# A graph convolution and a mixture of experts on one core: column means taken out of the first weights, keys and constants moved forward, degree roots written as rows, router rows on VectorE, low parts on GpSimd

## The chip, the core and the metric

The kernel runs as one program on one core of a Trainium2 chip. Its time is device microseconds of one execution on that core. TensorE multiplies matrices, VectorE, ScalarE and GpSimd compute element by element, each with a queue of its own that it works off in order; SyncE issues most DMA transfers, GpSimd the indirect ones.

## The reference, cut to what matters

```python
x: [1250, 512]          # nodes x features, float32
src, dst: [41250]       # edges, both directions and one loop of each node, sorted by dst

def gcn_conv(x, W, b, src, dst, n):        # adds another loop of each node to s and d
    h = x @ W.T
    deg = zeros(n).at[d].add(1.0)
    dinv = where(deg > 0, deg ** -0.5, 0)
    msg = h[s] * (dinv[s] * dinv[d])[:, None]
    return segment_sum(msg, d, n) + b

h = layernorm(x)                           # no weights
h = relu(gcn_conv(h, W1, b1))              # 512 -> 128
z = gcn_conv(h, W2, b2)                    # 128 -> 64
y = relu(z @ Wd1.T + bd1)                  # 64 -> 128
y = relu(y @ Wd2.T + bd2)                  # 128 -> 256
x = x + y @ Wd3.T + bd3                    # 256 -> 512

g = layernorm(x)                           # of the first 512 rows
# 512 tokens, 2 of 8 experts each (with weights), hidden 256, exact gelu:
for e in range(8):  y[rows of e] = gelu(g[rows of e] @ w1[e]) @ w2[e]
x[:512] += sum over a token's two experts of weight * y
return x
```

## The kernel before

The 1250 nodes are ten tiles of 128 rows (the last has 98). Because `dst` is sorted, the edges into six neighbouring nodes stand together: a *group* is six nodes, there are 209 groups, and the core gathers for each a window of 256 edges (`sg`, `dg`, indirect DMAs on GpSimd). The graph is turned into a dense count matrix `T` (source by target). For a group, VectorE compares edge keys with a row of numbers and so writes one-hot rows: `om` says of each edge which of 128 rows its source is (`source_rows`, L493), `on0` and `on1` say the tile of the source and the target (`target_rows`, L493 too). TensorE multiplies them (`count`, L521 and L524), ScalarE copies the counts out of PSUM (L532).

This runs in 14 steps, called *supers*, of sixteen groups, k = 0 to 13. Each has two halves, and the order of the other work around the counts is written by hand: `plan[(k, 0)]` and `plan[(k, 1)]` are the steps issued behind the first and the second half's counts, `plan[(k, 2)]` and `plan[(k, 3)]` those behind the pieces of the layers that follow. The source rows of super k + 1 are issued ahead of the counts of the first half of super k, its target rows ahead of those of the second half. So everything that a plan gives to VectorE stands in its queue between one-hot rows, and TensorE counts no faster than these come. In the plan are:

- the layer norm and the first product, tile by tile: `statistics` (VectorE, L287 and the line behind it: mean and variance into `mv`), `center` (ScalarE, L297: `xc` is the mean less x), `turned` (TensorE transposes `xc`, L308, ScalarE copies it out, L310), `product` (four matmuls with `W1s`, L317; a PSUM bank holds `PER` = 4 tiles);
- the degrees: `degree_rows` and `degree_sums`, `degree_row` (six row products on TensorE and three Sqrt on ScalarE for `rrow`, the roots as one row), `degree_inverse` (VectorE, and two DMAs on SyncE, which write 1/root to DRAM as `line` and read it back as rows into `drow`);
- `deviations` (ScalarE: `sd`), `scales` (VectorE) and `scaled_parts` (ScalarE multiplies the products by their scale), for each bank;
- the router of the experts: `router_pairs`, `router_ranks`, `router_places` (GpSimd, many small instructions), `router_lists` and `router_tokens`.

The products of `T` are made in bf16 with an operand cut into three parts that add up to float32 precision. `cut` makes them: ScalarE copies the high part, VectorE subtracts it (`low`, L446), ScalarE copies the middle part (L447), VectorE subtracts again (L448). `cut_on`, called in each half, issues the cuts that are due, two at most. `first_layer` puts its pieces into a list from which `fill` issues some behind each half, from super 4 on (`LAYER` = 4, 6, 8, 10, 12 are the supers behind which another chunk of 384 or fewer columns is ready): a matmul with the bias row `b1r` and `rrow`, ten parts of three or four matmuls (L560), a Relu, then the second product and the cut of `h2` in three parts (`h2hm` holds high and middle, `h2lo` the low part). The second layer multiplies the parts of `h2` with `T` (`thick` and `thin` pieces); then come the decoders `decode1` to `decode3`.

Behind the one-hot rows, in front of the second layer, GpSimd adds the last bias to all ten tiles of `xs` (`add_last_bias`, L1026). `decode3` adds its product to `xs`: for tiles 0 to 3 ahead of the experts, for tiles 4 to 9 at the end.

The experts' stage: the normalised rows of the 512 tokens go to DRAM (`x2d`), GpSimd fetches each expert's rows by indirect DMA into a ring of five buffers (`fetch`, L1148). Expert 0 comes by a product instead (`first_rows`). Each expert has up to 128 tokens in a tile of its own, and what it has above that in a tile shared by four (tiles 8 and 9). The order of the fetches is 8, 1, 2, 3, 4, 9, 5, 6, 7: five at once, each of the others behind the turn of an earlier one (`second_turn`, L1161, TensorE), since it needs its buffer. `results` multiplies by the second weights, and GpSimd scatters the scaled rows into `results_d` (a memset, L1219, and the indirect DMA, L1220); at the end they are read back and added.

```python
    gathers = [fetch(fetched.pop(0)) for _ in range(XG)]
    for i, e in enumerate(range(WAHEAD, WAHEAD + MORE)):
        for n, f in ((1, load_first), (2, load_second)):
            behind(f(e), gathers[2 * i + n], "behind rows that are wanted sooner")
    decode2(*c1)
    fill(len(pieces) // 2)
    first_rows()
```

(This is the place in the kernel, behind `decode3` of tiles 0 to 3, where the first five fetches are issued.)

Of the kernel before, what the change touches and what calls it, by code (L numbers as in the profile page):

```python
# [15 lines left out]
P = 128  # L16
# [32 lines left out]
def sorted_path(  # L49
# [110 lines left out]
    W1s = const.tile([P, KD, HID], F32)  # L160
# [53 lines left out]
    mv = const.tile([P, NT, 2], F32)  # L214
    deg = const.tile([P, NT], F32)
    root = const.tile([P, NT], F32)
    dcol = const.tile([P, NT], F32)
    hs = graph.tile([P, NT, HID], F32)
    h2 = graph.tile([P, NT, LAT], F32)
    if NF < NT:  # L220
        edge = rows(NF) // 32 * 32
        nc.vector.memset(mv[edge:, NF, :], 1.0)
        nc.vector.memset(dcol[edge:, NF:], 1.0)
        nc.vector.memset(root[edge:, NF:], 1.0)
        nc.vector.memset(deg[edge:, NF:], 0.0)
        nc.vector.memset(hs[edge:, NF, :], 0.0)
        nc.vector.memset(h2[edge:, NF, :], 0.0)
    lates = [graph.tile([P, SG, NK], F16, name=f"on1_{i}") for i in range(3)]
    for late in lates:
        nc.gpsimd.memset(late, 0.0)  # L230

# [9 lines left out]
    for c in range(2):  # L241
# [18 lines left out]
        for a, to in ((dst, dg), (src, sg)):  # L260
# [7 lines left out]
            )  # L268

# [11 lines left out]
    PER = 512 // HID  # L281
    products = [held_bank(f"ph{j}") for j in range((NT + PER - 1) // PER)]

# [5 lines left out]

    xTs = {}  # L290

    centered = {}

    def center(t):
        r = rows(t)
        centered[t] = work.tile([P, D], F32, tag="xc", name=f"xc{t}")
        nc.scalar.activation(  # L297
            centered[t][:r], xs[:r, t, :], AF.Identity, bias=mv[:r, t, 0:1], scale=-1.0
        )

    def turned(t):
        r = rows(t)
        if t not in centered:
            center(t)
        xc = centered.pop(t)
        pt = bank(f"pt{t}").rearrange("p (k r) -> p k r", k=KD)
        for k in range(KD):
            nc.tensor.transpose(pt[:, k, :r], xc[:r, k * P : (k + 1) * P], ident[:r, :r])  # L308
# [3 lines left out]
    def product(t):  # L312
        r = rows(t)
        xT = xTs.pop(t)
        to = products[t // PER][:r, (t % PER) * HID : (t % PER + 1) * HID]
        for k in range(KD):
            nc.tensor.matmul(to, xT[:, k, :r], W1s[:, k, :], start=(k == 0), stop=(k == KD - 1))  # L317
# [64 lines left out]
    line = dram.tile([NT * P], F32, name="line")  # L382
# [34 lines left out]
    def degree_row():  # L417
        for c, w in chunks:
            pr = bank(f"pr{c}")
            for h in range(HT):  # L420
                nc.tensor.matmul(
                    pr[0:1, :w], ones16, nodes[:, h, c : c + w], start=(h == 0), stop=(h == HT - 1)
                )
            nc.scalar.activation(rrow[:, c : c + w], pr[0:1, :w], AF.Sqrt, bias=ones[0:1])

    def degree_inverse():
        nc.vector.reciprocal(dcol, root)
        nc.vector.tensor_mul(dcol2, dcol, dcol)
        nc.sync.dma_start(out=line.rearrange("(t p) -> p t", p=P), in_=dcol)
        nc.sync.dma_start(  # L430
            out=drow, in_=bass.AP(tensor=line.tensor, offset=line.offset, ap=[[0, P], [1, N]])
# [33 lines left out]
    def deviations(a, b):  # L465
        nc.scalar.activation(sd[:, a:b], mv[:, a:b, 1], AF.Sqrt, bias=eps)

    def scales(a, b):
        nc.vector.reciprocal(scale[:, a:b], sd[:, a:b])
        nc.vector.scalar_tensor_tensor(  # L470
            scale[:, a:b], scale[:, a:b], -1.0, dcol[:, a:b], op0=OP.mult, op1=OP.mult
        )

    def scaled_parts(j):
        ts = range(j * PER, min(NT, (j + 1) * PER))
        for t in ts:
# [3 lines left out]
                products[j][:r, (t - ts[0]) * HID : (t - ts[0] + 1) * HID],  # L480
# [3 lines left out]
        cut(hs[:, s, :], [q[:, s, :] for q in hp], f"h{j}", j < 2)  # L484
# [82 lines left out]

    def first_layer(c, w):
# [3 lines left out]
        def part(t):  # L572
            if t == 0:
                box["ps"] = bank(f"l1_{c}")
                nc.tensor.matmul(
                    box["ps"][:, :w], b1r, rrow[:, c : c + w], start=True, stop=False
                )
            spread(box["ps"], c, w, t, [(q, HID) for q in hp], False, t == NT - 1)
# [4 lines left out]
        def second():  # L583
# [13 lines left out]
            cut(h2[:, s, :], [h2hm[:, s, :LAT], h2hm[:, s, LAT:], h2lo[:, s, :]], f"g{c}")  # L597
# [45 lines left out]
    def late_constants():  # L643
        for c in range(2):
            nc.vector.tensor_copy(
                iota_d[:, c], iota_m[:, :GN].unsqueeze(1).broadcast_to([P, HT * CG, GN])
            )
        nc.vector.memset(iota_d[:, 0, CG:, :LATE], -1.0)
        nc.vector.memset(iota_d[:, 1, CG:LASTG, :LATE], -1.0)

    statistics(0)
    center(0)
    statistics(1)
    center(1)
    first_keys = keys(0)
    turned(0)
    turned(1)
    statistics(2)
    late_constants()
    first_keys = more_keys(0, *first_keys)  # L660
    turn_keys(0, *first_keys)
    late_keys = keys(1)
    center(2)
    product(0)
    product(1)
    made = {0: (source_rows(*supers[0]),)}
    statistics(3)
    turned(2)
    made[0] = (*made[0], *target_rows(*supers[0]))
    center(3)  # L670
    product(2)
    turned(3)
    late_keys = more_keys(1, *late_keys)
    statistics(4)
# [179 lines left out]

    def router_places():
# [46 lines left out]
        pool.tensor_add(chunks_of[:, :, 1], chunks_of[:, :, 1], none[:, :TT])  # L902
        in_chunk = const.tile([P, BL, ST], BF16, name="in_chunk")
        for b in range(BL):
            pool.tensor_scalar(
                at_row[:, b, :], iota_m, at[:, b : b + 1], None, op0=OP.is_equal
            )
            pool.tensor_scalar(
                in_chunk[:, b, :], iota_m[:, :ST], chunk[:, b : b + 1], None, op0=OP.is_equal
            )  # L910
        pool.tensor_tensor(
# [36 lines left out]
    zero = graph.tile([P, D], F32)  # L948

# [7 lines left out]
    def both(f, *ts):  # L957
# [3 lines left out]
    groups = [(a, min(NT, a + PER)) for a in range(0, NT, PER)]  # L961
    plan = {
        (0, 0): both(product, 3) + [lambda: turn_keys(1, *late_keys)] + both(center, 4),
# [785 lines left out]
```

## Time and profile before

| | |
|---|---|
| median of 9 runs | 173.95 us (171.91 to 175.53) |
| the profiled execution: its own time | 173.5 us |
| its span in the profile | 171.7 us |
| mean granted clock of TensorE | 0.972 |
| TensorE busy with matmuls | 139.9 us (81%), 1236 instructions |
| TensorE loading weights (beside them) | 99.5 us (58%) |
| VectorE busy | 98.7 us (58%) |
| ScalarE busy | 69.2 us (40%) |
| GpSimd busy | 104.1 us (61%) |

The span is the time between the first and the last recorded instruction; the execution's own time has 1.8 us around it. A share of busy time is a mean over stages with different limits: VectorE is busy without a pause in the first 73 us and little behind them, TensorE the other way round. In a view, "L493" is the line of the code, and an arrow as in `on<-iota_n,keys_n` leads from what is read to what is written. Rows of the timeline give the start and the duration of one instruction in us, in square brackets how long its engine had been idle before it and what ended that. In the windows, each engine has its busy time with the number of instructions in it, then come the granted clock (1.00 is full speed), the DMA engines' share and GB/s.

### The profile page before, as it was taken

What the parts mean: (1) busy time and instruction counts of PE and PEld (TensorE: products, weight loads), DVE (VectorE), ACT (ScalarE), POOL (GpSimd) and SP (SyncE); (2) the same over time, 40 slices, a digit from 0 to 9 for tenths busy, and PEclk for the clock granted to TensorE, in tenths of its full rate; (3) what the DMA queues carried; (4) which work ended last, traced back from release to release, by engine and by line L of the source; (5) the groups of instructions that cost most, each with busy time, mean ns of one, the idle gap of its engine ahead of it and who ended that gap; (6) DMA issues with size and microseconds to landing.
All of it is one profiled execution on the core that took longest, in us unless ns stands there. A gap on an engine that the chain in (4) does not pass through costs nothing.

```text
span 171.7 us, 3271 instructions
## 1 busy us (share of the span) xinstructions
PE 139.9 (81%) x1236; PEld 99.5 (58%) x1236; DVE 98.7 (58%) x180; ACT 69.2 (40%) x154; POOL 104.1 (61%) x168
## 2 busy tenths in 40 slices
PE   0059838869988898899999999989799999999800
PEld 0048828867566797786434459769465993445200
DVE  5799999991999999914465780240113010314930
ACT  3078594889834545533213265412311312121000
POOL 8589989994999999999998001757206101540000
PEclk9999996999999999999999999999999999999975
DMA  5978420102543456341000033479997920349990
GB/s 166 329 173 284 135 93 0 1 6 84 191 122 122 126 142 229 150 155 65 4 0 0 0 122 122 133 233 295 376 374 245 323 108 0 124 183 316 391 363 34
DMA packets 18366, 27.13 MB, mean 158 GB/s; under 512 B 4312, under 2 KB 9177, under 8 KB 18344
## 3 DMA queue, kind: packets, MB, share of 16 engines
q1 hardware_dynamic: 16596, 21.38, 37.8%
q0 software_dynamic: 1712, 5.41, 9.2%
q8 instruction: 11, 0.18, 0.5%
q14 instruction: 11, 0.09, 0.2%
q10 hardware_dynamic: 36, 0.06, 0.2%
HBM read 18.52 MB, written 8.33 MB: 156 GB/s over the span
## 4 chain that ended last, share of the span: by engine, by line
DVE 29%; PE 28%; issue 16%; DMA 9%; ACT 7%; POOL 5%; ACTq 1%; DVEq 0%; POOLq 0%; SPq 0%
DVE om L493 12%; PE l L560 7%; DVE on L493 5%; PE pd L1097 4%; POOL results_d L1220 4%; DMA xg<-x2d,tokens 3%; PE pf L1178 3%; PE eh L1195 3%; DMA win<-in_dst_dram 3%; DVE xs L1329 2%; DMA x<-results_d 2%; PE pt L308 2%; PE pd L1088 2%; DVE st L287 2%; ACT xc L297 2%
## 5 line engine op out<-in xcount | busy, mean ns | idle before, releaser
L493 DVE TENSOR_TENSOR om<-iota_m,keys_m 128x4096 f16<-128x4096 f16 (+1 forms) x14 | 29.9, 2138 | 0.0
L1220 POOL DMA_INDIRECT results_d<-y,targets x10 | 9.8, 978 | 24.5 <-ACT y L1216 15.8
L560 PE MATMUL l<-T,hp 128*128 128x192 bf16 (+5 forms) x180 | 20.3, 253 | 0.4 <-DVE hp L448 0.4
L308 PE MATMUL pt<-ident,xc 128*128 128x128 f32 (+1 forms) x40 | 7.5, 325 | 15.1 <-ACT xc L297 15.1
L532 ACT CAST T<-acc 128x480 bf16<-128x480 f32 (+1 forms) x27 | 14.7, 546 | 11.4 <-PE acc L524 10.4
L1211 PE MATMUL ey<-w,hT 128*128 128x512 f32 (+1 forms) x64 | 18.9, 598 | 0.0
L1195 PE MATMUL eh<-xgT,w 128*128 128x160 f32 x128 | 18.6, 300 | 0.0
L1097 PE MATMUL pd<-Wd3s,y 128*128 128x512 f32 (+1 forms) x40 | 18.0, 592 | 0.0
L1148 POOL DMA_INDIRECT xg<-x2d,tokens x9 | 8.7, 967 | 15.1 <-PE pf L1178 12.6
L1195 PEld LDWEIGHTS eh<-xgT,w 128*128 128x128 f32 x128 | 17.6, 190 | 0.2 <-issue 0.2
L560 PEld LDWEIGHTS <-hp 128*128 128x128 bf16 (+1 forms) x216 | 14.9, 97 | 3.6 <-issue 1.4
L521 PE MATMUL acc<-on,om 128*128 128x60 f16 x209 | 15.4, 190 | 0.1
L524 PE MATMUL acc<-on,om 128*128 128x60 f16 x209 | 15.1, 190 | 0.4 <-DVE on L493 0.4
L1218 DVE TENSOR_SCALAR y<-ey,wslot 128x512 f32<-128x512 f32 x5 | 3.8, 751 | 20.2 <-PE ey L1211 20.2
L308 PEld LDWEIGHTS pt<-ident,xc 128*128 128x128 f32 (+1 forms) x40 | 5.2, 164 | 16.0 <-issue 9.6
L521 PEld LDWEIGHTS <-om 128*128 128x128 f16 x209 | 13.7, 98 | 1.2 <-issue 0.8
L493 DVE TENSOR_TENSOR on<-iota_n,keys_n 128x960 f16<-128x960 f16 (+2 forms) x28 | 14.1, 542 | 0.0
L317 PE MATMUL ph<-W1s,xT 128*128 128x128 f32 (+1 forms) x80 | 12.7, 314 | 1.0 <-ACT xT L310 1.0
L524 PEld LDWEIGHTS <-om 128*128 128x128 f16 x209 | 12.7, 97 | 0.3 <-issue 0.2
L1026 POOL TENSOR_TENSOR xs<-xs,bd3s 128x512 f32<-128x512 f32 (+1 forms) x10 | 12.4, 1274 | 0.0
L317 PEld LDWEIGHTS ph<-W1s,xT 128*128 128x128 f32 (+1 forms) x80 | 11.6, 223 | 1.4 <-ACT xT L310 1.4
L1097 PEld LDWEIGHTS pd<-Wd3s,y 128*128 128x128 f32 (+1 forms) x40 | 7.5, 188 | 8.2 <-issue 7.7
(217 smaller groups left out, 275.0 us busy)
## 6 DMA issues: line engine op xcount, KB each, us to landing
w<-in_L_ffn_w_dram SPq DMA_DIRECT2D x16, 512.0 KB, 6.7
xs<-in_x_dram SPq DMA_DIRECT2D x9, 256.0 KB, 4.7
out_dram<-xs SPq DMA_DIRECT2D x9, 256.0 KB, 4.6
results_d<-zero SPq DMA_DIRECT2D x4, 512.0 KB, 2.7
x2d<-x SPq DMA_DIRECT2D x4, 256.0 KB, 2.0
x<-results_d SPq DMA_DIRECT2D x2, 512.0 KB, 4.0
got<-results_d SPq DMA_DIRECT2D x2, 512.0 KB, 5.4
win<-in_dst_dram SPq DMA_DIRECT2D x2, 336.0 KB, 3.7
```

Of the source, the lines that this page charges most:

```text
L308: nc.tensor.transpose(pt[:, k, :r], xc[:r, k * P : (k + 1) * P], ident[:r, :r])
L317: nc.tensor.matmul(to, xT[:, k, :r], W1s[:, k, :], start=(k == 0), stop=(k == KD - 1))
L493: nc.vector.tensor_tensor(to.rearrange("p j (a f) -> p j a f", f=4), iota.rearrange("p (a f) -> p a f", f=4).unsqueeze(1).broadcast_to([P, ...
L521: nc.tensor.matmul(acc[:, n0 : n0 + NK], om[:, (at + g) * HT, :], on0[:, at + g, :], start=True, stop=False)
L524: nc.tensor.matmul(acc[:, n0 : n0 + NK], om[:, (at + g) * HT + 1, :], on1[:, at + g, :], start=False, stop=True,)
L532: nc.scalar.copy(T[:, :, g0 * GN : (g0 + ng) * GN], acc[:, : ng * NK].rearrange("p (d t) -> p t d", t=NT),).ins
L560: nc.tensor.matmul(ps[row0 : row0 + m, a:b], s[:r, t, :m], moving, start=start and i == 0, stop=stop and i == len(order) - 1,)
L1026: pool.tensor_add(xs[:r, t, :], xs[:r, t, :], bd3s[:r])
L1097: nc.tensor.matmul(p3[:r], y2[c][:, k, t * P - c : t * P - c + r], Wd3s[:, k, :], start=(k == 0), stop=(k == K2 - 1),)
L1195: nc.tensor.matmul(ph[:, f, :], first_w[e][:, k, f * P : (f + 1) * P], xgT[:, k, e, :], start=(k == 0), stop=(k == KD - 1),)
L1211: nc.tensor.matmul(to, hT[e][:, f, a:b], second_w[e][:, f, :], start=(f == 0), stop=(f == KF - 1))
L1220: ins = pool.indirect_dma_start(out=results_d[:, :], out_offset=bass.IndirectOffsetOnAxis(ap=targets[:, j : j + 1], axis=0), in_=y, in_off ...
```

## The change

- The mean leaves the rows by way of the weights. `center_weights` multiplies `W1s` with a matrix of 1/512 (`portion`), which gives each column's mean in every row, and subtracts it: `W1c`. A 129th column of 1/512 makes the product give the row's mean besides. `center` is gone, `turned` transposes x itself, three tiles (`PER`) share a bank, and the tenth has a place of its own.
- `statistics` stays for tiles 0 to 2. For tiles 3 to 9 ScalarE copies the negative mean out of the product (`mean`) and takes the sum of squares of x less the mean (`square`, with `accum_out`).
- The four instructions for `iota_d` move ahead of the first keys, which stand right behind two turned tiles now.
- The scales come in two groups, tiles 0 to 5 at (1, 3) and 6 to 9 at (3, 3), in place of three.
- The roots: `degree_row` is gone; TensorE turns root and 1/root at once (`degree_lines`), ScalarE copies them out, and SyncE writes them as rows and reads `rrow` and `drow` back. The product with the bias row stands at the end of each chunk of the first layer, where it stood at its beginning.
- For the first three chunks of the first layer ScalarE copies the high part, and both subtractions go to GpSimd (`slow_low` at (10, 1), `slow_rest` at (13, 0)), with ScalarE's copy of the middle part between them (`slow_middle`). `cut` of the other parts gets another delay (its last argument).
- `router_ranks` and `router_places` move from (3, 0) to (7, 0). The one-hot rows of the router, 17 instructions at the end of `router_places`, become three on VectorE (`router_rows`), behind the last super. The memset of `zero` moves from VectorE at (5, 2) to GpSimd at the beginning.
- `add_last_bias` stays in its place for tiles 0 to 3; for tiles 4 to 9 it moves behind the first five fetches.

The core of the diff:

```diff
+    zero = graph.tile([P, D], F32)
+    nc.gpsimd.memset(zero, 0.0)
...
-    PER = 512 // HID
-    products = [held_bank(f"ph{j}") for j in range((NT + PER - 1) // PER)]
+    PER = 3
+    groups = [(a, min(NT, a + PER)) for a in range(0, NT, PER)]
+    HM = HID + 1
+    products = [held_bank(f"ph{j}") for j in range(3)]
+    product_last = graph.tile([P, HM], F32)
+
+    def center_weights():
+        cm = bank("cm")[:, :HID]
+        for k in range(KD):
+            nc.tensor.matmul(cm, portion, W1s[:, k, :], start=(k == 0), stop=(k == KD - 1))
+        nc.vector.tensor_sub(W1c[:, :, :HID], W1s, cm.unsqueeze(1).broadcast_to([P, KD, HID]))
...
+    def mean(t):
+        r = rows(t)
+        nc.scalar.mul(nmean[:r, t : t + 1], made_product(t)[:r, HID:], -1.0)
+
+    def square(t):
+        r = rows(t)
+        junk = graph.tile([P, D], BF16, tag="square", name=f"square{t}")
+        nc.scalar.activation(
+            junk[:r],
+            xs[:r, t, :],
+            AF.Square,
+            bias=nmean[:r, t : t + 1],
+            accum_out=squares[:r, t : t + 1],
+        )
...
     def deviations(a, b):
-        nc.scalar.activation(sd[:, a:b], mv[:, a:b, 1], AF.Sqrt, bias=eps)
+        if a == 0:
+            nc.scalar.activation(sd[:, a:b], mv[:, a:b, 1], AF.Sqrt, bias=eps)
+        else:
+            nc.scalar.activation(sd[:, a:b], squares[:, a:b], AF.Sqrt, bias=eps, scale=1.0 / D)
...
-        cut(hs[:, s, :], [q[:, s, :] for q in hp], f"h{j}", j < 2)
+        cut(hs[:, s, :], [q[:, s, :] for q in hp], f"h{j}")
...
+    SLOW = [k * SG * GN for k in LAYER[:3]]
+    slow_cuts = []
+
+    def slow_low():
+        for s in slow_cuts:
+            nc.gpsimd.tensor_sub(h2[:, s, :], h2[:, s, :], h2hm[:, s, :LAT])
+
+    def slow_middle():
+        for s in slow_cuts:
+            nc.scalar.copy(h2hm[:, s, LAT:], h2[:, s, :])
+
+    def slow_rest():
+        for s in slow_cuts:
+            nc.gpsimd.tensor_sub(h2lo[:, s, :], h2[:, s, :], h2hm[:, s, LAT:])
...
-            cut(h2[:, s, :], [h2hm[:, s, :LAT], h2hm[:, s, LAT:], h2lo[:, s, :]], f"g{c}")
+            if c < SLOW[-1]:
+                nc.scalar.copy(h2hm[:, s, :LAT], h2[:, s, :])
+                slow_cuts.append(s)
+            else:
+                cut(h2[:, s, :], [h2hm[:, s, :LAT], h2hm[:, s, LAT:], h2lo[:, s, :]], f"g{c}", 1)
...
     plan = {
...
+        (0, 0): [lambda: turn_keys(1, *late_keys)] + both(product, 4) + both(turned, 5),
+        (0, 2): both(statistics, 0),
+        (0, 1): both(product, 5) + both(turned, 6) + both(mean, 3, 4),
+        (0, 3): both(degree_rows, 0, 1) + both(statistics, 1),
+        (1, 0): [degree_sums] + both(product, 6) + both(turned, 7) + both(mean, 5) + both(square, 3, 4),
+        (1, 2): both(statistics, 2),
+        (1, 1): both(product, 7)
+        + both(turned, 8)
+        + both(square, 5)
+        + [lambda: deviations(*groups[0]), lambda: deviations(*groups[1])],
+        (1, 3): [degree_inverse, lambda: scales(groups[0][0], groups[1][1])],
+        (2, 0): both(product, 8) + both(turned, 9) + both(scaled_parts, 0) + both(mean, 6, 7),
+        (2, 1): both(product, 9) + [degree_lines] + both(square, 6, 7) + both(mean, 8),
+        (3, 0): both(scaled_parts, 1)
+        + both(square, 8)
+        + [lambda: deviations(*groups[2])]
+        + both(mean, 9),
+        (3, 1): both(square, 9) + [lambda: deviations(*groups[3])],
+        (3, 3): [lambda: scales(groups[2][0], NT)],
         (4, 0): both(scaled_parts, 2),
+        (4, 1): both(scaled_parts, 3),
+        (7, 0): [router_ranks, router_places],
     }
...
-    for t in range(NT):
+    router_rows()
+    for t in range(TT):
         add_last_bias(t)
...
             behind(f(e), gathers[2 * i + n], "behind rows that are wanted sooner")
+    for t in range(TT, NT):
+        add_last_bias(t)
     decode2(*c1)
```

## The prediction

> **What bounds it now.** I began with busy time by stretch, from the view of windows (columns: TensorE, its weight loads, VectorE, ScalarE, GpSimd, granted clock, DMA share).
>
> ```profile
> 30.00:40.00 10.00, 7.82 (x115) 7.43 (x115) 8.73 (x16) 8.47 (x20) 9.45 (x20) 1.00 0.10 3
> 40.00:50.00 10.00, 9.36 (x101) 5.85 (x97) 7.49 (x10) 7.63 (x20) 7.56 (x12) 1.00 0.49 155
> ...
> 60.00:73.00 13.00, 11.54 (x216) 10.43 (x213) 13.00 (x19) 6.94 (x19) 12.68 (x10) 1.00 0.51 173
> 73.00:88.00 15.00, 14.37 (x161) 9.15 (x157) 5.07 (x9) 4.16 (x15) 14.92 (x21) 1.00 0.17 63
> ...
> 130.00:150.00 20.00, 20.00 (x122) 13.55 (x115) 3.38 (x5) 3.95 (x8) 5.29 (x10) 1.00 0.44 153
> ```
>
> Up to 73 us VectorE makes one-hot rows without a pause, but TensorE has almost as much to do (11.54 of 13.00), so a gain on VectorE alone does not all come through. Behind 73 us TensorE sets the pace, wholly so from 130 to 150. Next, the timeline of VectorE, for its pauses inside the first stretch, and GpSimd beside it:
>
> ```profile
> 37.81 1.05 DVE L493 TENSOR_TENSOR on<-iota_n,keys_n 128x960 f16<-128x960 f16 x2
> 42.48 0.71 DVE L448 TENSOR_TENSOR hp<-lowh,hp 128x512 bf16<-128x512 f32 x1 [3.62 <-ACT hp L447]
> 52.11 2.28 DVE L493 TENSOR_TENSOR om<-iota_m,keys_m 128x4096 f16<-128x4096 f16 x1
> 52.38 2.07 POOL L887 TENSOR_TENSOR at<-at,batch 128x8 f32<-128x8 f32 x1
> ```
>
> VectorE has one pause, 3.62 us, and ScalarE, late with its queue, causes it. The two lower rows overlap: a GpSimd instruction on eight columns, 0.20 us elsewhere, stands still while source one-hots run. Last, I followed GpSimd past the graph, and TensorE's wait for what it fetches:
>
> ```profile
> 111.94 0.95 POOL L1148 DMA_INDIRECT xg<-x2d,tokens  x1 [0.30 <-issue]
> 112.89 0.09 POOL L1219 MEMSET between<- 1x1 f32 x1
> 114.19 1.01 POOL L1220 DMA_INDIRECT results_d<-y,targets  x1 [1.22 <-DVE y L1218]
> 115.51 0.97 POOL L1148 DMA_INDIRECT xg<-x2d,tokens  x1 [0.31 <-PE qt L1161]
> 123.28 0.63 PE L1161 MATMUL qt<-ident,xg 128*128 128x128 f32 x4 [1.17 <-DMA xg<-x2d,tokens]
> ```
>
> The fifth fetch of token rows is issued at 111.94, the sixth at 115.51; the sixth (the shared tile 9) lands 7.6 us later, and TensorE, which turns it ahead of expert 3, already waits 1.17 us for it. There is no slack there.
>
> **The change, VectorE's queue.** Times are starts in the timeline, an instruction's cost the step to the next start. Ahead of the one-hots three statistics (2.4) go, the four constants move forward, and subtracting the column means (512 columns out of PSUM, as `L1076`: 0.69) comes in. All that ends by about 10.0, but `hi` needs the first `sg` gather, issued at 7.46 and landing 3.80 later: 11.3 instead of 11.59, so −0.3. From there to the first `scale` (30.39 before) six statistics at 0.82 become three: ready at 30.39 − 0.3 − 2.5 = 27.6.
>
> There a new wait stands. The scales of tiles 0 to 5 need the deviation of tile 5, which ScalarE now makes from a square. No row has a square with a sum. By `L297` it steps 0.62; the read of the sum lies between nothing and 0.4 (VectorE's read of a sum is 0.08, ScalarE's one-column instruction `L1125` 0.29); I take 0.95 with its wait for the mean. A mean is 0.10 to 0.29, I take 0.15 (`L415`). From the T copy at about 24.7 ScalarE then has: T 0.5, roots and degrees 0.6, a pause for tile 7's transposes 0.7, its copy 0.5, a mean 0.15, two squares 1.9, T 0.5, copy of tile 8 0.5, square 5 0.95, two deviations 0.3: 31.3 at the end, 31.0 with the overlaps. VectorE waits 3.4 us and begins the next source rows at 31.4; before it was 30.67. Behind it 3.65 (2.2 source, 1.0 target, 0.46 low part of three tiles) brings 35.05, before 35.01. Then 2.2 + 0.46 + 1.0 + 0.46 bring 39.1, where the scales of tiles 6 to 9 wait in the same way: from a T copy at 33.4 the queue is T copies 3 × 0.46, the last product and the turned roots 0.55, squares 6 to 9 3.8, means 0.3, middle part 0.4, three scaled tiles and their high part 1.4, deviations 0.4: 8.2, so 41.6, and 41.4 with overlaps. The next source rows begin at 41.8 (43.38 before): 1.6 us gained, where the plain ledger would give more. In all ScalarE loses eight centrings (5.0) and three root rows (1.5) in this stretch and gains 7.7: the engine that VectorE waited for is not relieved.
>
> From 43.38 to the last target rows at 73.1 it was 29.7. The cuts of three chunks leave VectorE (0.27 + 0.27 + 0.14 + 0.13 + 0.20 + 0.30 = 1.3), `zero` too (0.4); the cuts of h keep their sum (3.2). So 41.8 + 28.0 = 69.8: VectorE ends 3.3 us sooner. The router's rows come later on VectorE, three instructions of 1024, 80 and 480 elements, 1.2 by the rate of `om` (2.2 for 4096) to 3.0 by plain steps, in its pause behind 73 us, where it waited 3.04 for `lowg`; without that cover they would delay the next low part.
>
> **TensorE.** Three more transposes' worth of work (column means, roots) against six row products (1.29 at 41.04) is small. Its first layer cannot start before the low parts of groups 0 and 1, which stand behind source rows ending at 44.0: 44.5, where it was 44.36 behind the bias product, now moved to the end of each chunk. So it begins no sooner and gains only where it waited for VectorE. Bounds: −3.3 (it follows wholly), 0 (it does not); I take −2.0. The DMA of turned roots adds one issue on SP; if its write took as long as the old one (10.1 until the next issue), the root row would still land near 48, ahead of its first use near 52.
>
> **GpSimd.** `router_ranks` moves from slot (3, 0) to (7, 0), some 57.3. Of the 27 instructions behind it, 22 took 43.52 to 64.80 before, 0.97 each under the one-hots; nine small ones at 91.42 to 93.49 took 0.26 each. 12.5 us until 69.8 do 13, the other 14 at 0.28 take 3.9: 73.7. Three low subtractions on 384 columns, by `L1026` (1.24 for 512), 1.0: 74.8; ScalarE's three middle copies end at 75.2. They stand in its queue ahead of the Relu of chunk 960, wanted at 77.19 − 2.0 = 75.2. I take +0.3; at 0.97 for all it would be 83.5 + 1.5, +8; below nothing it can't be.
>
> **Bias rows, moved past a queue.** Six `add_last_bias` (1.24 each, 7.4) leave the stretch at 79 to 91, where GpSimd was idle afterwards anyway (12.6 us until the first fetch), and now stand behind the fifth fetch. Queued behind them are the memset, the first scatter and fetches six to nine. The sixth goes out at 112.89 + 7.4 + 1.7 (memset, scatter with its start, start of the fetch) = 122.0, +6.5. Landing was 4.2 to 7.6 after issue, median 6.1; the 7.6 belonged to a full DMA stretch, and part of the weights will have passed by then, so I take 6.1: the rows come 6.5 − 1.5 = 5.0 later (bounds 3.1 and 6.5), and since TensorE waits there already and runs full until 150, all of it shows at the end. After the longer wait the array starts slowly: behind waits of 2.11 and 0.91 us at 22 to 26 the granted clock was
>
> ```profile
> 26.00:28.00 2.00, 2.00 (x10) 2.00 (x11) 2.00 (x2) 0.88 (x2) 1.83 (x3) 0.50 0.00 0
> ```
>
> and eight products took 1.91 instead of 1.06, four transposes 1.12 instead of 0.66; with the matmuls beside them I take +1.5 (0 to 2).
>
> [...]
>
> Sum: 173.5 (the profiled execution; span 171.7) − 2.0 + 0.3 + 5.0 + 1.5 = 178.3. That execution lies 0.45 under the median of 173.95, which I leave.
>
> **Rivals.** First, faster: ScalarE is in time for both scales (a square costs no more than a centring). Then VectorE keeps its whole ledger: start 0.3, four statistics 3.3, cuts 1.3, zero and a scale pair 0.7, the pause 3.6, together 9.2. If all reached TensorE: 173.5 − 9.2 + 6.5 = 170.8; it decides once the graph's gain passes 6.5. For it speaks the 3.62; against it TensorE's 11.54 of 13 and ScalarE's ledger. Second, same: a gain of 5 in the graph and late rows at their lower bound without a clock loss (3.1 to 5) cancel, about 173. Third, the moved bias rows cost nothing, because tile 9 is not what TensorE wants: 173.5 − 1.7 = 171.8; the 1.17 us row speaks against it. Fourth, GpSimd is late with the low parts, ScalarE's queue stands still behind it, and nothing of the second layer can start: +4 to +8, near 184; for it speaks that a blocked instruction takes 2.07.
>
> **Chances.** Forecast 0.55; first rival 0.12, second 0.11, third 0.05, fourth 0.17. I give 178.3 and the range 171.5 to 183.0: the second and third rivals and the lower half of the fourth are in it, the first below, the worst GpSimd above. About 1% is what a measurement of this kernel can tell from no change; faster by more is 0.15 (first rival and most of the third), within it 0.13 (the second and the rest of the third), slower 0.72. Cases of both signs lie in the range; the forecast's own is 175.5 to 181.0.
>
> **What will show it.** In the changed profile: VectorE waiting some 3 us for `sd` ahead of the fourth source rows and some 2 ahead of the sixth; its last target rows near 69.8; the three ScalarE copies of the middle parts ending near 75; six `add_last_bias` between the fifth and sixth fetch; TensorE waiting about 6 us for `xg` in front of expert 3, with a low clock behind it. I am wrong if that wait stays near 1 us, or if the graph part ends more than 5 us sooner.

## The result, and the profile after

The changed kernel takes 184.07 us (median of 20 executions, 179.95 to 187.5), the kernel before 174.92 (62 executions, 171.91 to 178.07): 9.15 us slower; the ratio is 1.042 with an interval of 1.0372 to 1.0468 (it compares undisturbed executions alone, hence less than the medians' 1.052). The profiled execution of the changed kernel took 178.84 us (span 177.1, mean clock 0.947), less than any of the 20. So there are two questions: what made the profiled one 5.3 us slower than that of before (173.5), and what lies between it and the median.

The windows of the changed kernel, in the stretches that were shown of before (TensorE, its weight loads, VectorE, ScalarE, GpSimd, granted clock, DMA share, GB/s):

```profile
30.00:40.00 10.00, 5.53 (x98) 4.71 (x98) 8.11 (x11) 9.81 (x33) 9.87 (x14) 0.95 0.18 66
40.00:50.00 10.00, 7.83 (x77) 4.82 (x74) 9.55 (x14) 5.36 (x16) 7.43 (x12) 0.88 0.34 107
...
60.00:73.00 13.00, 11.94 (x230) 11.04 (x231) 9.76 (x12) 6.80 (x18) 11.81 (x22) 1.00 0.53 180
73.00:88.00 15.00, 14.35 (x153) 9.12 (x150) 7.42 (x13) 4.82 (x18) 11.81 (x24) 1.00 0.16 60
...
130.00:150.00 20.00, 20.00 (x130) 14.69 (x129) 2.79 (x4) 3.52 (x8) 3.15 (x6) 0.97 0.35 121
```

VectorE has room now (9.76 of 13 in the third row), but TensorE is as full there as before (11.94), and fuller than nine tenths in the next. Between 30 and 50 TensorE does less and its clock is below 1.00, where it was 1.00 before. VectorE's timeline shows the two waits for the deviation that ScalarE makes, a pause for TensorE's counts (`acc`), and the end of the one-hot rows:

```profile
30.79 0.19 DVE L508 RECIPROCAL scale<-sd 128x6 f32<-128x6 f32 x1 [2.33 <-ACT sd L505]
...
40.41 0.18 DVE L508 RECIPROCAL scale<-sd 128x4 f32<-128x4 f32 x1 [1.48 <-ACT sd L505]
...
56.39 2.29 DVE L530 TENSOR_TENSOR om<-iota_m,keys_m 128x4096 f16<-128x4096 f16 x1 [1.09 <-PE acc L561]
...
69.48 0.28 DVE L530 TENSOR_TENSOR on<-iota_n,keys_n 128x60 f16<-128x60 f16 x2
...
86.91 0.69 DVE L1120 TENSOR_TENSOR z<-l,drow 128x512 f32<-128x512 f32 x1 [2.97 <-PE l L597]
```

The last row is the first latent product, behind the whole graph stage: 86.91, where it was 87.27 before. VectorE's one-hots end 3.3 us sooner, the graph stage 0.4.

TensorE begins the first layer at 40.17 and stands still for VectorE for the last time ahead of 47.84; ScalarE copies the middle parts at 75.19:

```profile
40.17 1.15 PE L597 MATMUL l<-T,hp 128*128 128x384 bf16 x3
...
47.84 1.15 PE L597 MATMUL l<-T,hp 128*128 128x384 bf16 x6 [1.81 <-DVE hp L483]
```

```profile
75.19 0.70 ACT L616 CAST h2hm<-h 128x192 bf16<-128x192 f32 x3
```

GpSimd, and TensorE behind it, in the experts' stage:

```profile
111.57 0.94 POOL L1192 DMA_INDIRECT xg<-x2d,tokens  x1 [0.30 <-issue]
112.53 7.42 POOL L1069 TENSOR_TENSOR xs<-xs,bd3s 128x512 f32<-128x512 f32 x6
119.90 0.09 POOL L1263 MEMSET between<- 1x1 f32 x1
120.15 1.02 POOL L1264 DMA_INDIRECT results_d<-y,targets  x1 [0.16 <-issue]
121.48 0.96 POOL L1192 DMA_INDIRECT xg<-x2d,tokens  x1 [0.31 <-PE qt L1205]
```

```profile
128.35 1.09 PE L1205 MATMUL qt<-ident,xg 128*128 128x128 f32 x4 [6.91 <-DMA xg<-x2d,tokens]
129.23 3.25 PE L1239 MATMUL eh<-xgT,w 128*128 128x160 f32 x16
132.32 5.45 PE L1255 MATMUL ey<-w,hT 128*128 128x512 f32 x24
137.71 0.66 PE L1205 MATMUL qt<-ident,xg 128*128 128x128 f32 x4
```

The six bias additions (7.42) stand between the fifth and the sixth fetch. The sixth goes out at 121.48 (115.51 before), and TensorE, which turns its rows, begins at 128.35 (123.28): 5.07 later. Then the array is slow: sixteen products of expert 3 take 3.25, 2.34 before, and from this turn to the next it is 9.36 where it was 8.02 (131.30 less 123.28). At the next turn the kernel is 6.4 behind, and about 1 of that comes back behind TensorE's last product (8.2 us to the end of the span, before 9.2).

### The profile page after: what moved, and what is told of

Same layout as the page of the kernel before. It is cut to its first block, busy times and chain, and to the rows that moved or that the text cites. A ratio compares the mean times of both kernels' runs of the same rounds, so it can differ in the third digit from the quotient of the medians.

```text
span 177.1 us, 3276 instructions
## 1 busy us (share of the span) xinstructions
PE 141.9 (80%) x1239; PEld 101.5 (57%) x1239; DVE 93.5 (53%) x165; ACT 67.9 (38%) x167; POOL 92.8 (52%) x158
## 4 chain that ended last, share of the span: by engine, by line
PE 65%; ACT 11%; DVE 10%; DMA 5%; issue 3%; POOL 1%; DVEq 0%; POOLq 0%; ACTq 0%
PE l L597 14%; PE eh L1239 11%; PE ey L1255 10%; PE pd L1141 8%; DMA xg<-x2d,tokens 4%; PE ph L350 3%; PE qt L1205 3%; PE pf L1222 3%; ACT square L327 3%; PE pd L1132 3%; DVE om L530 2%; PE acc L558 2%; PE acc L561 2%; PE p L644 2%; PE l L631 2%
## 5 line engine op out<-in xcount | busy, mean ns | idle before, releaser
L597 PE MATMUL l<-T,hp 128*128 128x192 bf16 (+5 forms) x180 | 22.1, 264 | 2.0 <-DVE hp L483 2.0
L1239 PE MATMUL eh<-xgT,w 128*128 128x160 f32 x128 | 19.7, 310 | 0.0
L558 PE MATMUL acc<-on,om 128*128 128x60 f16 x209 | 16.4, 195 | 3.9 <-DVE on L530 3.7
L1239 PEld LDWEIGHTS eh<-xgT,w 128*128 128x128 f32 x128 | 18.6, 199 | 0.4 <-ACT xgT L1213 0.2
L597 PEld LDWEIGHTS <-hp 128*128 128x128 bf16 (+1 forms) x216 | 16.0, 102 | 4.6 <-DVE hp L483 2.7
L558 PEld LDWEIGHTS <-om 128*128 128x128 f16 x209 | 14.7, 102 | 5.3 <-DVE on L530 4.4
L561 PE MATMUL acc<-on,om 128*128 128x60 f16 x209 | 15.9, 194 | 0.6 <-DVE on L530 0.6
L561 PEld LDWEIGHTS <-om 128*128 128x128 f16 x209 | 13.6, 100 | 0.5 <-issue 0.4
L341 PE MATMUL pt<-ident,xs 128*128 128x128 f32 (+1 forms) x40 | 6.9, 302 | 7.5 <-DMA xs<-in_x_dram 7.4
L1255 PEld LDWEIGHTS ey<-w,hT 128*128 128x128 f32 (+1 forms) x64 | 6.9, 149 | 9.2 <-issue 8.4
L350 PE MATMUL ph<-W1c,xT 128*128 128x129 f32 x72 | 10.1, 283 | 1.6 <-ACT xT L343 1.6
L1205 PE MATMUL qt<-ident,xg 128*128 128x128 f32 x36 | 5.8, 293 | 6.9 <-DMA xg<-x2d,tokens 6.9
```

What stands on the lines that cost most here:

```text
L350: nc.tensor.matmul(to[:r], xT[:, k, :r], W1c[:, k, :], start=(k == 0), stop=(k == KD - 1))
L558: nc.tensor.matmul(acc[:, n0 : n0 + NK], om[:, (at + g) * HT, :], on0[:, at + g, :], start=True, stop=False)
L561: nc.tensor.matmul(acc[:, n0 : n0 + NK], om[:, (at + g) * HT + 1, :], on1[:, at + g, :], start=False, stop=True,)
L597: nc.tensor.matmul(ps[row0 : row0 + m, a:b], s[:r, t, :m], moving, start=start and i == 0, stop=stop and i == len(order) - 1,)
L1205: nc.tensor.transpose(pt[:, k, :], xg[j][:, k * P : (k + 1) * P], ident)
L1239: nc.tensor.matmul(ph[:, f, :], first_w[e][:, k, f * P : (f + 1) * P], xgT[:, k, e, :], start=(k == 0), stop=(k == KD - 1),)
```

## The experiments

Medians are compared with the kernel before on the same chip.

### The bias additions alone

```diff
 # the kernel before
-    for t in range(NT):
+    for t in range(TT):
         add_last_bias(t)
...
+    for t in range(TT, NT):      # behind the first five fetches
+        add_last_bias(t)
     decode2(*c1)
```

> The kernel before with nothing but the six bias additions moved behind the first five fetches. Both theories: TensorE waits 6 to 7 us for the sixth fetch's rows; 173.5 + 5.1 + 1.4 less about 1 at the end, where the last stores have room, 179 in the profile. Theory C: the median is 174.9 + 6, about 181, since the graph stage is that of before. Theory D: about 184, with the spread of the changed kernel (8 us).

Measured: 183.33 against 176.14, ratio 1.0542 (1.0451 to 1.0633). The moved additions alone make the kernel before slower by 7.2 us (by the ratio 5.4%, some 9). Its profiled execution took 183.66:

```profile
131.00 1.09 PE L1161 MATMUL qt<-ident,xg 128*128 128x128 f32 x4 [6.47 <-DMA xg<-x2d,tokens]
...
141.40 0.66 PE L1161 MATMUL qt<-ident,xg 128*128 128x128 f32 x4
```

Its graph stage ended 2.45 later than in the first profile of before, with the same code: the graph's end moves by that much from one execution to the next. The rest is the wait (6.47), and a stretch of 10.40 to the next turn, where the changed kernel had 9.36. Rows that land late (theory D) explain little of the spread: in the seven profiles with the additions moved and no unread matmuls ahead of this turn, tile 9 was turned 6.1 to 7.3 us after the issue of its fetch.

And the other way round, the changed kernel with the additions put back:

```diff
 # the changed kernel
-    for t in range(TT):
+    for t in range(NT):
         add_last_bias(t)
...
-    for t in range(TT, NT):
-        add_last_bias(t)
```

> The changed kernel with all ten bias additions ahead of the lists again, as before; all else as changed. Theory C (clock): the six moved additions cost 6.4 us in every execution (5.1 of landing, 1.4 of low clock behind the wait), and what lies between the profiled 178.84 and the median of 184.07 is TensorE at half clock behind its pauses in the graph stage, in other places in each execution. Then the sixth fetch goes out near 115, the profile gives 172.5 to 173.5, the median falls by about 6.4 to 177.7, and its executions still lie 5 us or more apart. Theory D (transfers): the spread comes from rows that land late beside the weights. Then it goes with the wait: a median near 174 to 175, within 3 us.

Measured: 176.79 against 176.14, ratio 1.0145 (1.0039 to 1.025). The wait for tile 9 is 0.8 again. So everything else in the change, some 300 lines of it, is worth nothing or costs a little. The profile shows something that neither theory had in it. GpSimd, ScalarE and TensorE in the graph stage:

```profile
59.45 11.42 POOL L902 TENSOR_TENSOR ranks<-ranks,oh 128x64 f32<-128x64 f32 x1 [17.53 <-ACT ranks L897]
```

```profile
78.61 0.95 ACT L616 CAST h2hm<-h 128x192 bf16<-128x192 f32 x3 [2.45 <-POOL h L612]
```

```profile
79.98 0.66 PE L644 MATMUL p<-W2s,h1T 128*128 128x64 f32 x4 [2.32 <-ACT h1T L636]
```

One GpSimd instruction on 64 columns takes 11.42 us, from 59.45 to 70.87; VectorE's last one-hots run at 70.59. GpSimd's 26 small instructions behind it then follow in 7.1 us, the low parts come at 78.03 instead of 73.92, ScalarE's queue stands 2.45 for them and TensorE 2.32 for ScalarE. In the profiled execution of the changed kernel the same instruction took 0.83:

```profile
58.58 0.83 POOL L902 TENSOR_TENSOR ranks<-ranks,oh 128x64 f32<-128x64 f32 x1 [10.73 <-ACT ranks L897]
```

### The clock

At this point one theory for the spread was TensorE at half clock behind its pauses. The profile after has such stretches (windows of one us; the clock stands third from the end):

```profile
38.00:39.00 1.00, 0.69 (x16) 0.60 (x17) 0.93 (x3) 0.97 (x5) 1.00 (x3) 0.96 0.32 115
39.00:40.00 1.00, 0.72 (x17) 0.61 (x14) 0.00 (x0) 1.00 (x3) 0.87 (x6) 0.50 0.00 0
...
52.00:53.00 1.00, 0.76 (x5) 0.76 (x6) 1.00 (x2) 0.19 (x1) 0.00 (x0) 0.79 0.93 324
...
124.00:125.00 1.00, 0.00 (x0) 0.00 (x0) 0.00 (x0) 0.00 (x0) 0.94 (x1) 0.63 1.06 354
...
131.00:132.00 1.00, 1.00 (x9) 1.00 (x8) 0.00 (x0) 0.00 (x0) 0.00 (x0) 0.95 0.00 0
```

Matmuls that nothing reads were put where TensorE paused:

```diff
+    def warm(n):
+        for _ in range(n):
+            nc.tensor.matmul(products[2][:, 400:512], ident, ident[:, :112], start=True, stop=True)
...
-        (2, 1): both(product, 9) + [degree_lines] + both(square, 6, 7) + both(mean, 8),
+        (2, 1): both(product, 9) + [degree_lines, lambda: warm(4)] + both(square, 6, 7) + both(mean, 8),
...
-        (3, 1): both(square, 9) + [lambda: deviations(*groups[3])],
+        (3, 1): both(square, 9) + [lambda: deviations(*groups[3]), lambda: warm(12)],
...
+            if c == 0 and t == 6:      # in part(t) of first_layer
+                warm(8)
...
+            if j == NE + 1:            # in turn_next, 30 of them
+                for _ in range(30):
+                    nc.tensor.matmul(spare[0], ident, ident[:, :112], start=True, stop=True)
             second_turn(j)
```

All four places, on the changed kernel:

> The changed kernel with matmuls that nothing reads (128x112, float32) where TensorE paused: 4 ahead of the counts of super 3, 12 ahead of those of super 4, 8 ahead of part 6 of the first layer's first chunk, 30 ahead of the turn of tile 9. Theory C: no stretch at half clock up to 160 us, graph stage up to 2 us shorter, nothing lost behind the wait (1.4): 175.5 to 177 in the profile, a median of 177 to 178, within 4 us. Theory D: a profile of about 178 and a median of about 184, spread as in the changed kernel.

Measured: 179.06 against 176.14, ratio 1.0311 (1.0232 to 1.039); six executions from 178.5 to 185.28. The median is above the 177 to 178 of the clock theory, with no changed kernel beside it on this chip, and the spread did not narrow; nor did the matmuls do all that was asked of them, since the profile still has half clock from 54.6 to 58.1.

The first three places, with the additions ahead:

> The changed kernel with all ten bias additions ahead of the lists, and the first three groups of unread matmuls (24 in all). Theory C: the graph stage ends 2 us sooner than before, 170.5 to 172 in the profile, a median of 171 to 173, faster than the kernel before by 1 to 2%. Theory D: no different from the first of these runs.

Measured: 176.97 against 176.14 (172.59 to 179.15). No gain over the same kernel without them (176.79 beside it), though the clock was 1.00 from 30 to 75 us; and the ranks' instruction was held for 11.42 again. What the matmuls took away is half clock from 39.8 to 46.6, which costs nothing that can be seen; in the fifties, where it does cost (below), both profiles were at full clock.

The fourth place alone, on the changed kernel:

```diff
+            if j == NE + 1:
+                for _ in range(30):
+                    nc.tensor.matmul(spare[0], ident, ident[:, :112], start=True, stop=True)
```

> The changed kernel with nothing but the 30 unread matmuls ahead of the turn of tile 9. In four profiles the stretch from that turn to the next took 9.4, 10.4, 11.0 and 10.5 us behind a cold wait, 8.0 to 8.1 without one. Theory C for this place: 8.0 in the profile, the median lower by 1.3 to 3, the landing as late as ever. If the half clock there is hidden by later waits: no change.

```profile
132.03 0.63 PE L1205 MATMUL qt<-ident,xg 128*128 128x128 f32 x4
...
140.06 0.66 PE L1205 MATMUL qt<-ident,xg 128*128 128x128 f32 x4
```

The stretch is 8.03 again, as expected, but the median is 181.83 against 174.56 (1.0341, 1.0248 to 1.0435), not below the 181.29 of the changed kernel on that chip. The profiled execution had the held instruction (11.42), its first latent product at 90.89. So the clock's part is shown in the stretch, and not in the median.

The changed kernel itself, beside it:

> The changed kernel itself, for a comparison on one chip with the next three: a median of 183 to 185; if the profile shows the first instruction of the ranks held until the last one-hots, its first latent rows are 5 to 6 us later than in the first profile (86.9).

181.29 against 174.56, six executions from 180.52 to 181.85; the instruction took 0.54 in this profile, the stretch behind tile 9 9.50.

### GpSimd held back

If GpSimd is held by VectorE's unbroken run, starting it sooner should help:

```diff
-        (7, 0): [router_ranks, router_places],
+        (5, 0): [router_ranks, router_places],
```

With the additions late, as changed:

> The changed kernel with router_ranks and router_places at (5, 0) instead of (7, 0); the six bias additions stay behind the fetches. Theory G (GpSimd locked out): in two profiles the first GpSimd instruction of the ranks took 11.42 us, until VectorE's last one-hots, in two others 0.47 and 0.83; where it is held, the low parts and the router's rows come 4 us later and the first latent rows 5 to 6. Started 10 us sooner, even a held instruction leaves the low parts in time or nearly so: a median of 179 to 180 and a profile of 178 to 179, no clock needed. Theory C (clock) and theory D (landing): the median stays at 183 to 184.

Measured: 181.84 against 175.6 (1.0366, 1.0268 to 1.0463), with two of six executions at 186.1 and 188.0: a miss of 2 us for theory G (that GpSimd is locked out). The profiled graph stage was as in the first profile, but the stretch behind tile 9 took 10.99 (127.98 to 138.97).

With the additions ahead:

> The changed kernel with all ten bias additions ahead of the lists and router_ranks, router_places at (5, 0). Theory G: both losses gone, a median of 173 to 174 against 176.8 with the additions alone put back. Theory C: no different from that, 176.8.

Measured: 173.11 against 175.6, ratio 0.9846 (0.9746 to 0.9945). This looked like a version better than both; the repetition below does not bear it out.

With the unread matmuls too:

> The one before it, with the 24 unread matmuls in TensorE's three pauses of the graph stage. Theory C and G together: 171.5 to 172.5, faster than the kernel before by 1.5 to 2.5%. G alone: no different from the one before it, within 0.5 us.

Measured: 173.33 against 175.6. No different from the one before it. That does not take the clock out as a cause: the profile without the matmuls was at half clock from 38.3 to 45.1 only, where TensorE waits for VectorE anyway. What half clock costs later two traces show, by the second products (`W2s`) of the first two chunks. The changed kernel, at half clock from 52.6 to 56.0:

```profile
52.24 1.26 PE L644 MATMUL p<-W2s,h1T 128*128 128x64 f32 x6 [0.58 <-ACT h1T L636]
...
60.22 0.43 PE L644 MATMUL p<-W2s,h1T 128*128 128x64 f32 x2 [0.42 <-ACT h1T L636]
```

The run before this one (additions ahead, ranks early), at full clock there:

```profile
53.33 0.88 PE L644 MATMUL p<-W2s,h1T 128*128 128x64 f32 x6 [0.58 <-ACT h1T L636]
...
59.65 0.43 PE L644 MATMUL p<-W2s,h1T 128*128 128x64 f32 x2 [0.42 <-ACT h1T L636]
```

7.98 us against 6.32. Of the sixteen profiles of the changed kernel and its variants eight were at half clock there (7.9 to 8.0) and eight were not (6.3 to 6.4).

The cuts on VectorE again (the changed kernel otherwise):

```diff
-            if c < SLOW[-1]:
+            if False:
                 nc.scalar.copy(h2hm[:, s, :LAT], h2[:, s, :])
                 slow_cuts.append(s)
             else:
                 cut(h2[:, s, :], [h2hm[:, s, :LAT], h2hm[:, s, LAT:], h2lo[:, s, :]], f"g{c}", 1)
```

> The changed kernel with the cuts of the first three chunks on VectorE again; ranks at (7, 0) and bias additions as changed. Theory G, if the harm goes by way of the low parts and ScalarE's queue: VectorE ends 1.3 us later (near 71), no ScalarE copy waits for GpSimd, a median near 180. If it goes by way of the router's rows too, which VectorE makes from GpSimd's places: 182 to 183. Theories C and D: 184 to 185.

Measured: 181.09 against 175.6 (1.035, 1.0287 to 1.0414), six executions within 2.2 us. This lies between the two readings, and the instruction was not held in its profile (0.31), so it does not tell by which way the harm goes.

The direct test is to give GpSimd a pause. One VectorE copy of one column waits for the ranks' instruction, between two of VectorE's one-hot instructions:

```diff
-        pool.tensor_mul(ranks, ranks, oh)
+        pool.tensor_mul(gated, ranks, oh)
...
+    plan[(8, 1)] = [lambda: nc.vector.tensor_copy(seen, gated[:, 0, 0:1])]
```

With the additions ahead:

> The changed kernel with all ten bias additions ahead of the lists (ranks at (7, 0)), and one VectorE copy of a single column that waits for GpSimd's first ranks instruction, between the target rows of super 9 and the source rows of super 10. Theory G says a pause of VectorE lets the held instruction go: it takes under 3 us in the profile, the low parts are in time, and the median falls from 176.8 to 173.5 to 175. If it is held for another reason than VectorE's run, VectorE now waits for it and the median rises to 180 or more.

```profile
57.95 1.67 POOL L904 TENSOR_TENSOR gated<-ranks,oh 128x64 f32<-128x64 f32 x1 [12.86 <-ACT ranks L897]
```

```profile
59.66 0.15 DVE L1037 COPY seen<-gated 128x1 f32<-128x1 f32 x1 [0.20 <-POOL gated L904]
```

Measured: 172.79 against 174.56, twelve executions from 171.48 to 175.42 (ratio 1.0028, 0.9973 to 1.0083, so no faster than before by that measure). A VectorE pause of 0.20 us was enough: the instruction ended with it, at 59.62.

The last four ran on one chip (before: 174.89). The changed kernel a third time:

> The changed kernel, beside the next three on one chip: 181 to 184 by all theories.

182.37 (1.0503, 1.0411 to 1.0595). This time its own profile has the held instruction, and the profiled execution took 183.72, close to the median:

```profile
58.16 11.42 POOL L902 TENSOR_TENSOR ranks<-ranks,oh 128x64 f32<-128x64 f32 x1 [12.86 <-ACT ranks L897]
```

```profile
89.95 0.69 DVE L1120 TENSOR_TENSOR z<-l,drow 128x512 f32<-128x512 f32 x1 [2.97 <-PE l L597]
```

```profile
131.61 1.09 PE L1205 MATMUL qt<-ident,xg 128*128 128x128 f32 x4 [7.13 <-DMA xg<-x2d,tokens]
...
142.22 0.66 PE L1205 MATMUL qt<-ident,xg 128*128 128x128 f32 x4
```

Beside the first profile (178.84): the latent product 3.0 later, tile 9 3.3 later, the stretch to the next turn 10.61 instead of 9.36, so 4.5 at that point, of 4.9 in all.

The changed kernel with VectorE's one waiting copy:

> The changed kernel with nothing but the one VectorE copy that waits for GpSimd's first ranks instruction (between the target rows of super 9 and the source rows of super 10). If that instruction, held in some executions, is what lies between the quickest executions of the changed kernel and its median: a median 2 to 4 us under the changed kernel's on this chip, 178 to 180, within 3 us. If the spread comes from the half clock behind the wait for tile 9 alone: no lower, with the same spread.

180.97, 1.4 under the changed kernel beside it, instruction 0.79, latent product 87.97. The sign is as theory G has it, the size half of it, and six executions each leave room.

> The changed kernel with all bias additions ahead of the lists: 5 to 7 us under the changed kernel on the same chip, and within 1 us of the kernel before.

175.66: 6.7 under the changed kernel, and 1.0037 (0.9979 to 1.0095) of the kernel before. In its profile the instruction was held for 11.60.

> Bias additions ahead and ranks at (5, 0): 2 to 4 us under the run before this one if the held instruction is the graph's loss, and faster than the kernel before by 1 to 2%; within 1 us of the run before this one if it is not.

173.89: 1.8 under the one before it, but 1.0006 (0.9939 to 1.0072) of the kernel before. With the additions ahead and the ranks early the change is as good as before, perhaps 1% better; a clear gain it is not.

### The squares

```diff
 # additions ahead, ranks at (5, 0)
-        (0, 2): both(statistics, 0),
+        (0, 2): both(statistics, 0, 3),
...                                       # and so on: no mean, no square
+        (2, 2): both(statistics, 6, 7),
+        (2, 3): both(statistics, 8, 9),
```

> Bias additions ahead, ranks at (5, 0), and the statistics of tiles 3 to 9 on VectorE again, without the squares. VectorE gets 7 times 0.82 and loses the two waits for the deviations (2.3 and 1.5): its last target rows 1.9 us later, near 71.7. If VectorE set the graph's pace, 1 to 2 us slower than the same kernel with squares (173.1); if TensorE does, since it paused for VectorE only between 33 and 48 us, within 0.5 us of it.

Measured: 175.16 against 174.56 (0.9968, 0.9895 to 1.004). Its last one-hots were at 71.09 in the profile and the ranks' instruction was held for 9.36, until VectorE paused for TensorE. Its median is 1.3 above that of the same kernel with squares on this chip (173.89, just above), but the ratios, 0.9968 and 1.0006, show no difference; and if there is one, this run does not tell whether VectorE's work makes it or the held instruction.

## Why the prediction was wrong

Point by point, first against the profiled execution, on which the sum was built (178.3 forecast, 178.84 measured).

- **VectorE's queue: right.** Waits for `sd` of 2.33 and 1.48 (3.4 and 2.4 forecast), the source rows behind them at 31.10 and 40.71 (31.4 and 41.8), last target rows ending at 69.76 (69.8). That the end fits so well is luck: the second start was 1.1 early, and a pause of 1.09 for TensorE's counts at 56.39, which no term had, took it back.
- **TensorE's gain, −2.0: too much.** It was −0.4. The reading that TensorE begins the first layer no sooner than 44.5 was wrong: it began at 40.17, since a chunk begins with the first three tiles, whose low part was done at 37.50, and for that of the next three it waited only 0.17. But it paused 2.70 and 1.81 (`on`, `hp`), and from 47.84 on the chain that ends last runs over TensorE and ScalarE's Relus, not over VectorE: TensorE was busy 11.94 of 13.00 and 14.35 of 15.00, with next to nothing to give back. VectorE's 3.3 us stayed in VectorE's queue. And the half clock from 52.6 to 56.0 made TensorE's way longer by 1.66 (7.98 against 6.32), about what the term lacks.
- **Bias rows, +5.0: right in mechanism, half a us small.** The turn of tile 9 came 5.07 later, but that has the graph's −0.4 in it, which the sum counts apart: the term itself is 5.5. The fetch went out 6.0 later, as 6.5 less the graph's 0.4 has it, and its rows landed 0.9 quicker, not 1.5.
- **Low clock behind the wait, +1.5 (0 to 2): a term too small.** 1.34 in the first profile, but 1.5, 1.9, 2.4, 2.5, 2.6 and 3.0 in six others, 2.2 in the mean. In the first profile the granted clock fell to 0.50 at 124.3, 2.8 us after TensorE's last matmul, and came back 6.8 us later, at 131.1; in the kernel before with nothing but the additions moved it was 0.50 for 6.8 too, but from some 129.1, 4.6 us after the last matmul, to 135.9; with the ranks at (5, 0), the dearest of the seven, it came back at 134.0 only, after 7 or more. Sixteen products of expert 3, 2.34 in the kernel before, took 3.25 to 4.47 in the seven. What sets the beginning and the length of such a stretch no run here tells. One profiled pause, which was the source of my bounds, could not show that range.
- **GpSimd, +0.3 (bounds 0 and +8): the step that failed.** In the profiled execution it was as computed: low parts done at 75.1, middle copies ending at 75.9 (75.2 forecast), nothing queued behind them late. But I made a duration out of a mean, 0.97 for each instruction under the one-hots, and took a middle for the certain case. The instruction is either through soon (0.31 to 0.83) or held until VectorE's one-hots end (11.42 or 11.60, in five of nine profiles with the ranks at (7, 0)); at (5, 0) it took 0.72 to 1.17 in four profiles and 9.36 in one, until VectorE paused. Held, the graph stage ends 3.2 to 4.8 us later, counted from VectorE's last one-hots (20.65 to 22.24, against 17.4 in the first profile). With the additions ahead, the three profiled executions with it held for 11.42 or 11.60 took 176.56 to 178.63, the four with it through 171.56 to 172.91. That was the fourth rival, by its own mechanism and at the lower end of its 4 to 8; at 0.17 it was priced as a mishap, and it is an ordinary execution.
- **What the prediction and the experiments both left out: the two go together.** In all five profiles with the instruction held, TensorE was at full clock from 47 to 60 and VectorE worked without a break. In the four others it was at half clock for 3.4 us between 52 and 59, and VectorE paused (0.33 to 2.56) at the instruction or less than 3 us ahead of it. So these executions paid either the half clock or the held instruction. That the first spares the second is seen in nine profiles and tested by none.

So the forecast is the sum of one execution, in which the instruction went through and the clock behind the wait came back early. That it lies 0.5 from that execution is in part luck: the graph gave 1.3 less than the −1.7 of two terms, the bias term was 0.5 short, and the 1.0 that came back at the end stood in no term.

Against the medians the sum falls short by GpSimd's term first, and by the clock's. The moved additions (6.5 forecast, with the clock) cost 7.2 alone and 6.7 taken back, 5.4 and 4.6% by the ratios. All the rest (−1.7 forecast) came to +0.7 and +0.8 with the additions ahead (176.79 less 176.14, 175.66 less 174.89), and to −1.0 to −2.5 in the four medians with the instruction freed or started early; the ratios show less of this step (1.0145 and 1.0037 against 0.9846, 1.0006 and 1.0028). An estimate with the sizes that were measured: 173.5 − 0.4 + 5.5 + 2.2, and 1.8 for the held instruction (tile 9 comes 3.26 later in the third profile than in the first, taken five times in nine), make 182.6, less up to 1.0 at the end; 181.29 and 182.37 were measured in the later repetitions.

The held instruction with a longer half clock gives the 4.9 between the quick profile and the third one. That the second of these sets the median of the first 20 executions (184.07) is likely and not shown, since only profiled executions show the instruction; freeing it alone took 1.4 off the median, within what six executions leave open. Why that median lies 1.7 to 2.8 above the 181.29 and 182.37 stays open.

## What to carry to other kernels

Work that is moved off a crowded stretch onto a queue that issues transfers delays every transfer behind it (here the sixth fetch went out at 121.48 instead of 115.51): look up what is fetched next on that queue and who already waits for it, before counting the gain. An off-path engine beside one that works without a break may have no mean duration, as GpSimd's first ranks instruction at (7, 0) had none (0.31 to 0.83 us, or 11.42 and 11.60): price it as through at once and as held until the other pauses, and give it slack for the second, or put in a short wait that makes the other pause (0.20 us was enough here). And where a sum rests on one profiled execution, its terms that depend on luck want their own spread, since the median takes them at their middle.

## What the runs showed of the hardware

A GpSimd instruction stayed behind VectorE's f16 one-hots not for one of them but for a run of them: 11.42 us over three and a half supers, to the same hundredth in four executions, 11.60 in a fifth, and 9.36 in one where VectorE paused sooner. A wait for the one-hot instruction at hand alone would have ended some 0.53 us later in the five cases of 11.42 and 11.60: these began 0.52 to 0.53 us ahead of the end of a source one-hot instruction (59.45 against 57.70 and 2.28) and came through neither then nor at the next ones, but with the last, short one-hots or just behind them. A sixth, in the run with the waiting copy, began 0.54 ahead and came free with a VectorE pause of 0.20. Other cases would fit a wait for one instruction: three at (5, 0) that began 1.0 ahead of the end of source rows took 1.17, the first profile's, 0.10 ahead, 0.83, and those that began while target rows were written or VectorE stood still 0.31 to 0.79. But the one that took 9.36 began 1.0 ahead of such an end as well. By what the one engine holds the other, and why the ones that follow in GpSimd's queue get through in each super (in the kernel before, the six longest of those from 43.52 to 64.80 took 2.07 to 2.28 us), and this first one at times does not, no run here tells.
